# A two-layer local-attention block: another order for the instructions of its steps

## The chip, the core and the metric

The kernel runs on one core of a Trainium2 chip. The metric is the device time of one execution in microseconds; lower is better. A core has four computing engines that each execute their own list of instructions in order: PE (TensorE: matmuls, with weight loads, PEld, beside them), DVE (VectorE), ACT (ScalarE) and POOL (GpSimd). SP (SyncE) issues most DMAs. PE writes to PSUM only; DVE and ACT read PSUM, POOL works on SBUF. Engines wait for one another by semaphores.

## The reference, cut to what matters

The input x is (2, 1024, 256). A first part (attention with 16 heads under conditions, then a soft mixture of 64 experts) and a second part (a rotation of the features, then two layers of local attention with feed-forward) are each added to x. The change touches the second part alone:

```python
def _layer(x, wqkv, qs, ksc, wo, lg, lb, w1, b1, w2, b2):
    h = shift_token(x)
    q, k, v = split(h @ wqkv)                 # 8 heads of 64
    q, k = l2norm(q) * qs, l2norm(k) * ksc
    q, k = rotary_xpos(q, k)
    o = local_attention(q, k, v)              # windows of 128: own and previous one
    x = x + o @ wo
    h = shift_token(x)
    h = (h - mean) / sqrt(var + 1e-5) * lg + lb
    a, g = split(h @ w1 + b1)                 # 682 each
    x = x + (a * gelu(g)) @ w2 + b2
    return x
for l in range(2):
    x = _layer(x, ...)
```

All arithmetic is float32.

## The kernel before, in words

The second block works in windows of 128 tokens: 2 layers x 2 sequences x 8 windows = 32 windows, numbered through. A loop (line 1570 and on) runs over steps s = -2 to 31. In step s the queries, keys and values of window s + 2 are projected, window s + 1's queries and keys are turned to features by rows, window s is scored, exponentiated and divided by its sums, and the weights of windows s - 1 and s - 2 are turned and mixed with the values. Four windows make a chunk of 512 tokens; after its last window follows `project_out`, and the feed-forward of chunk f is spread over four steps by `forward(s - LAG)` with LAG = 7: gates 0 and 1, gates 2 and 3, gate 4 with `centre(f + 1)` and gate 5, then `normalise`, `normalised` and `feed`.

The whole loop stands in `tc.manual_schedule` for PE, DVE, ACT and POOL. So on these engines the instructions are executed in the order in which the Python code issues them; SP's are not in that list. The calls and what they issue:

- `project(i)`: 4 matmuls 128x512, each issued as two instructions (tile pq). `rotate_parts(i)`: ACT copies pq to raw and squares it (sq), DVE multiplies pq with the cosines (t, line 1162), POOL multiplies raw with the sines in two products (t, line 1182).
- `values(i)`: 2 matmuls (pv); `keep_values(i)`: ACT copy to v.
- `norms(i)`: DVE sums the squares (ss) and makes a first guess of the inverse root (z); POOL refines it in 12 small products (nt, zn). `rotated(i)`: DVE adds the two parts of t and multiplies the keys' half with the norms.
- `turn(i)`: 16 half transposes on PE (pt), ACT copies them to qkT, which has slots for three windows.
- `scores(i, hg)`: for each half of the heads, 64-row matmuls (sc). `maxima`: four DVE instructions (line 1268) that add the mask, scale by the queries' norm and find the largest. `weights`: four ACT exponentials with sums. `divide(i, 0)`: a DVE reciprocal and four POOL products; `divide(i, 1)`: the same, all on DVE.
- `turn_e(i, hg)`: 16 half transposes (pe), copied to eT by ACT (hg = 0) or DVE (hg = 1). `mix(i, hg)`: the 64-column matmuls po; after the second half ACT copies po into oT. The tile oT holds one chunk and has one buffer (pool `xin`, bufs = 1).
- `project_out(g)`: 8 matmuls (16 instructions, pwo), then DVE adds to xa and writes xb. `halves(g)`: POOL adds xb's two halves for the mean. `centre(f)`: the mean by PE (pm), two DVE differences (hc), an ACT square, a POOL sum. `gate(f, n)`: matmuls pga, ACT Gelu, DVE product. `feed(f)`: 24 matmul instructions py, then the sums into xa (layer 0) or the output (layer 1).

PSUM tiles of two banks (pq, sc, pe, pt, pwo, pga, py) come from `two_banks`. From the end of the mixture part on it hands out three such tiles in turn: every third from `ps_c`, the others from `ps_b` with two buffers. A tile that comes round again waits until all readers of its last use are done. Single banks (pv, po, pm, pvar) come from `ps_1` with two buffers.

A step is called `dense` (line 1586) when no mixture work stands beside it and it is not one of the last two: s = 5 to 29. Before the change all steps, dense or not, go through one body with conditions. A project_out stands in steps 5, 9, 13, 17, 21, 25 and 29. In step 5 there is no feed-forward yet, in step 6 `centre(0)` and `normalise(0)`. Step 13 also loads tables and projection weights of layer 1 (`weights2(1, "tabs", "wqkv")`), with four POOL products on the tables.

Of the kernel before, what the change touches and what calls it, by code (L numbers as in the profile page):

```python
# [10 lines left out]
F32 = mybir.dt.float32  # L11
# [6 lines left out]
P = 128  # L18
B = 2
# [72 lines left out]
def tile_kernel(ctx: ExitStack, tc: tile.TileContext, a: dict, out: bass.AP):  # L92
# [1003 lines left out]
    with tc.manual_schedule(  # L1096
# [41 lines left out]
        def project(i):  # L1138

            l, b, w = window(i)  # L1140
            pq = two_banks("pq")
            for x in range(2):
                for k in range(2):
                    nc.tensor.matmul(  # L1144
                        pq[:, x, :],
                        shifted(xa, k, b, w * WIN, P),
                        load["wqkv"][:, k, x * 512 : (x + 1) * 512],
                        start=(k == 0),
                        stop=(k == 1),
                    )  # L1150
            pqs[i] = pq.rearrange("p x (h d) -> p (x h) d", d=DH)
# [91 lines left out]
        def scores(i, hg):  # L1243

            at, wins = parts(i)
            lo = 0 if len(wins) > 1 else WIN
            sc = two_banks("sc").rearrange("p x (c k) -> p x c k", c=2)
            for c in range(2):
                for x in range(2):
                    r = slice(64 * x, 64 * x + 64)  # L1250
                    nc.tensor.matmul(  # L1251
                        sc[:, x, c, lo:],
                        qkT[r, 0, 2 * hg + c, i % 3, :],
                        qkT[r, 1, 2 * hg + c, at, :],
                        start=True,
                        stop=True,
                    )
            scs[i, hg] = sc, lo, 2 if len(wins) > 1 and wins[0][1] == i else 0
# [153 lines left out]
        def gate(f, n, between=None):  # L1412

            l = chunk(f)[0]
            if n == 0:
                us[f] = fa["u"]
            pt = two_banks("pga")
            gl = fa["gl"][:, gates[0] % 2, :]
            gates[0] += 1
            if n < NW1:  # L1420
                for x, lo in ((0, W1G + n * P), (1, W1A + n * P)):
                    for k in range(2):
                        nc.tensor.matmul(  # L1423
                            pt[:, x, :], load["w1"][:, k, lo : lo + P], hcs[f][:, k, :], start=(k == 0), stop=(k == 1)
                        )
# [13 lines left out]
            if n == NW1:  # L1439

                nc.gpsimd.tensor_copy(us[f][TG : TG + TAIL, n, :], us[f][:TAIL, n, :])
# [69 lines left out]
                nc.vector.scalar_tensor_tensor(yo, py, col(f"b2{l}", c), yo, ALU.add, ALU.add)  # L1511
                nc.sync.dma_start(out[c * P : (c + 1) * P, b * S + t0 + lo : b * S + t0 + lo + m], yo)

        def forward(at):

            f, k = divmod(at, 4)
            if at == -1:
                normalise(0)
            if not 0 <= f < CHUNKS:
                return  # L1520
            if k == 0:
                gate(f, 0)
                gate(f, 1)
            if k == 1:
                gate(f, 2)
                gate(f, 3)
            if k == 2:
                gate(f, 4)
                if f + 1 < CHUNKS:
                    centre(f + 1)  # L1530
                gate(f, 5)
            if k == 3:
                if f + 1 < CHUNKS:
                    normalise(f + 1)
                    normalised(f + 1)
                feed(f)


# [28 lines left out]

        LAG = 7
        fa = {}
        for s in range(-2, WINDOWS):  # L1570
            now, before, nxt, new = (0 <= s + d < WINDOWS for d in (0, -1, 1, 2))

            if new:
                project(s + 2)
                rotate_parts(s + 2)

            if s == LAG - 1:
                centre(0)
            if s == LAG:
                normalised(0)  # L1580
            ended = 0 <= s - 2 < WINDOWS

            late = s >= WINDOWS - 2
            dense = s > max(PARTS) and not late
            if ended and not dense and not late:
                mix(s - 2, 1)
            if now and dense:
                for hg in range(2):  # L1590
                    scores(s, hg)
            if ended and dense:
                for hg in range(2):
                    if (s - 2, hg) in eTs:
                        mix(s - 2, hg)
            if s == 5:
                rotate(3)
            if now and not dense and not late:
                scores(s, 0)
                maxima(s, 0)  # L1600
            beside(s, "a")
            if before:
                turn_e(s - 1, 0)
            if now and not late:
                if dense:
                    maxima(s, 0)
                weights(s, 0)
            if new:
                values(s + 2)
                keep_values(s + 2)  # L1610
            beside(s, "c")
            if ended and late:
                for hg in range(2):
                    if (s - 2, hg) in eTs:
                        mix(s - 2, hg)
            if now:
                for hg in () if dense else (0, 1) if late else (1,):
                    scores(s, hg)
                for hg in (0, 1) if late else (1,):
                    maxima(s, hg)  # L1620
                    if hg == 0:
                        weights(s, 0)
            if before and not dense:
                mix(s - 1, 0)
            if nxt:
                turn(s + 1)
            if now:
                weights(s, 1)
            if new:
                norms(s + 2)  # L1630
            if s + 2 == B * NWIN - 1:
                weights2(1, "tabs", "wqkv")
            beside(s, "b")
            if 0 <= s - 2 < WINDOWS and (s - 2) % 4 == 3:
                project_out((s - 2) // 4)
                if (s - 2) // 4 in halved:
                    halves((s - 2) // 4)
            if before:
                turn_e(s - 1, 1)
            if now:  # L1640
                divide(s, 0)
            if new:
                rotated(s + 2)
            if s == 5:

                f = xp.tile([P, 4 * NS], F32, tag="e", name="f")
                at = 0
                for name, k, n in (("u", NF, 512), ("w2", NF, D), ("yo", 2, 512), ("rs", 1, 512), ("sq", 2, 512), ("gl", 2, 512)):
                    fa[name] = f[:, at : at + k * n].rearrange("p (k n) -> p k n", k=k)
                    at += k * n  # L1650
                fa["rs"] = fa["rs"][:, 0, :]
                fa["hc"] = xin.tile([P, 2, 2, 512], F32, tag="x1", name="hc")
                load["w2"] = fa["w2"]
                load["w1"] = xp.tile([P, NE // 4 * D], F32, tag="y1", name="w1")[:, : 2 * W1N].rearrange(
                    "p (k n) -> p k n", k=2
                )
                weights2(0, "w1", "w2")
            forward(s - LAG)
            if now:
                divide(s, 1)  # L1660
            beside(s, "e")
            if s == B * NWIN + 2:
                weights2(1, "wo")
            if s == LAG + 4 * (CHUNKS // 2) - 2:
                weights2(1, "w1")
            if s == LAG + 4 * (CHUNKS // 2) - 1:
                weights2(1, "w2")


        w, f = WINDOWS - 1, CHUNKS - 2  # L1670
# [136 lines left out]
```

## Time and profile before

| | us |
|---|---|
| median of 3 runs | 1572.27 (1572.12 to 1572.6) |
| the profiled execution | 1572.25 |
| its span | 1570.2 |
| busy in it: PE, DVE, ACT, POOL | 1553.9, 905.7, 891.9, 539.6 |
| step s = 12 (gates 2 and 3), from its first pq to the next | 18.02 |
| step s = 13 (project_out, gate 4, centre, gate 5) | 24.36 |
| step s = 14 (normalise, feed) | 21.75 |

The steps in the trace are found by the first matmul of pq: s = 5 begins at 968.45, s = 6 at 989.57, s = 12 at 1102.95, s = 29 at 1445.79. A row of the timeline has the start and the duration in us, the engine, the line, the operation, output and inputs by the program's names, partitions x elements and the number of instructions merged; in brackets stands the idle time of the engine before it and who ended it. A row of the waits has who waited for whom, the total in us, how often, and the longest. A merged row's duration ends with the last result, so for how long a group holds PE one takes the start of the next row.

### The profile page before, as it was taken

What the parts mean: (1) busy time and instruction counts of PE and PEld (TensorE: products, weight loads), DVE (VectorE), ACT (ScalarE), POOL (GpSimd) and SP (SyncE); (2) the same over time, 40 slices, a digit from 0 to 9 for tenths busy, and PEclk for the clock granted to TensorE, in tenths of its full rate; (3) what the DMA queues carried; (4) which work ended last, traced back from release to release, by engine and by line L of the source; (5) the groups of instructions that cost most, each with busy time, mean ns of one, the idle gap of its engine ahead of it and who ended that gap; (6) DMA issues with size and microseconds to landing.
All of it is one profiled execution on the core that took longest, in us unless ns stands there. A gap on an engine that the chain in (4) does not pass through costs nothing.

```text
span 1570.2 us, 24701 instructions
## 1 busy us (share of the span) xinstructions
PE 1553.9 (99%) x9664; PEld 762.4 (49%) x9664; DVE 905.7 (58%) x1606; ACT 891.9 (57%) x1678; POOL 539.6 (34%) x835
## 2 busy tenths in 40 slices
PE   8999999999999999999999999999999999999999
PEld 4333433333333444444776666555555554545544
DVE  5868768776873122125455756656575665657532
ACT  2478768787886222226233654766757575666641
POOL 3333323333330100000102345555565555565411
PEclk9999999999999999999999999999999999999999
DMA  5100010000000544445742102000100001000001
GB/s 163 55 14 14 1 21 8 7 15 8 2 1 28 169 144 142 148 158 186 239 122 81 55 1 83 1 1 1 67 2 1 15 1 56 1 1 28 14 14 40
DMA packets 49860, 82.79 MB, mean 53 GB/s; under 512 B 4552, under 2 KB 25200, under 8 KB 49488
## 3 DMA queue, kind: packets, MB, share of 16 engines
q1 hardware_dynamic: 47200, 75.38, 15.6%
q0 software_dynamic: 1584, 5.29, 1.1%
q8 instruction: 76, 1.25, 0.3%
q10 hardware_dynamic: 960, 0.56, 0.1%
q14 instruction: 40, 0.33, 0.1%
HBM read 56.04 MB, written 20.97 MB: 49 GB/s over the span
## 4 chain that ended last, share of the span: by engine, by line
PE 96%; DVE 2%; DMA 1%; ACT 0%; POOL 0%; issue 0%; ACTq 0%; DVEq 0%; POOLq 0%
PE pga L1423 9%; PE sc L344 9%; PE po L362 8%; PE pm L310 7%; PE lg L813 7%; PE cmb L932 7%; PE sl L839 7%; PE pq L1144 6%; PE py L1450 4%; PE pv L1214 4%; PE pwo L1354 4%; PE po L1334 3%; PE sc L1251 3%; PE pe L1229 2%; PE pqk L280 2%; PE py L860 2%
## 5 line engine op out<-in xcount | busy, mean ns | idle before, releaser
L317 DVE TENSOR_REDUCE mx<-pm 128x2 f32<-128x1024 f32 x256 | 301.5, 1220 | 108.0 <-PE pm L310 107.8
L352 ACT ACTIVATE e<-sc 128x512 f32<-128x512 f32 (+1 forms) x500 | 263.6, 613 | 67.7 <-PE pm L310 63.5
L344 PE MATMUL sc<-qs,km 32*128 32x512 f32 x1024 | 247.7, 616 | 0.7 <-ACT cg L562 0.7
L310 PE MATMUL pm<-km,qm 32*128 32x512 f32 x1024 | 242.8, 616 | 0.0
L380 POOL TENSOR_TENSOR ob<-ob,part 128x512 f32<-128x512 f32 x101 | 128.6, 1273 | 251.1 <-ACT part L379 251.1
L1423 PE MATMUL pga<-hc,w 128*128 128x512 f32 x320 | 143.8, 600 | 0.0
L1301 POOL TENSOR_SCALAR e<-e,den 128x256 f32<-128x256 f32 (+1 forms) x128 | 131.2, 1038 | 26.3 <-DVE den L1297 26.2
L362 PE MATMUL po<-e,v 128*32 128x512 f32 x1024 | 136.8, 604 | 0.0
L344 PEld LDWEIGHTS sc<-qs,km 32*128 32x128 f32 x1024 | 91.6, 183 | 86.6 <-ACT e L352 65.2
L1182 POOL TENSOR_TENSOR t<-raw,tabs 128x512 f32<-128x512 f32 x64 | 80.6, 1280 | 142.5 <-ACT raw L1174 142.3
L1285 ACT ACTIVATE e<-e,nmx 128x256 f32<-128x256 f32 (+1 forms) x256 | 123.6, 488 | 3.8 <-DVE nmx L1268 3.5
L932 PE MATMUL cmb<-xb,y 128*128 128x256 f32 x512 | 118.7, 384 | 0.6 <-ACT xb L918 0.6
L1144 PE MATMUL pq<-wqo,xa 128*128 128x512 f32 x256 | 116.4, 597 | 1.9 <-ACT xb L918 1.2
L813 PE MATMUL lg<-phi,xa 128*128 128x512 f32 x256 | 116.1, 595 | 0.0
L839 PE MATMUL sl<-dsp,xb 128*128 128x512 f32 x256 | 114.9, 592 | 0.0
L310 PEld LDWEIGHTS pm<-km,qm 32*128 32x128 f32 x1024 | 83.2, 183 | 49.2 <-DVE mx L317 34.9
L823 DVE TENSOR_TENSOR l<-lg,keep 128x512 f32<-128x512 f32 x32 | 22.1, 692 | 144.8 <-ACT keep L821 144.8
L1268 DVE CUSTOM_DVE_ANT_0 e<-sc,mask,zn 128x256 f32<-128x256 f32 (+1 forms) x256 | 102.0, 462 | 5.4 <-PE sc L1251 5.4
L932 PEld LDWEIGHTS cmb<-xb,y 128*128 128x128 f32 x512 | 94.9, 189 | 17.9 <-issue 3.2
L1174 ACT COPY raw<-pq 128x1024 f32<-128x1024 f32 x32 | 32.4, 1013 | 107.8 <-PE pq L1144 106.7
L1423 PEld LDWEIGHTS pga<-hc,w 128*128 128x128 f32 x320 | 58.9, 190 | 68.0 <-issue 63.8
L821 ACT COPY keep<-lg 128x512 f32<-128x512 f32 x32 | 18.7, 585 | 126.0 <-issue 105.3
(225 smaller groups left out, 2384.1 us busy)
## 6 DMA issues: line engine op xcount, KB each, us to landing
lgd<-keep SPq DMA_DIRECT2D x64, 256.0 KB, 2.4
w<-in_ffn_W SPq DMA_DIRECT2D x16, 1024.0 KB, 7.0
ebig<-lgd SPq DMA_DIRECT2D x64, 256.0 KB, 3.3
wqo<-in_wqkv SPq DMA_DIRECT2D x2, 1536.0 KB, 8.1
w<-in_w SPq DMA_DIRECT2D x2, 1386.0 KB, 6.5
km<-hk SPq DMA_DIRECT2D x32, 64.0 KB, 2.3
qm<-hq SPq DMA_DIRECT2D x32, 64.0 KB, 2.3
phi<-in_phi SPq DMA_DIRECT2D x1, 2048.0 KB, 7.7
```

Of the source, the lines that this page charges most:

```text
L310: nc.tensor.matmul(pm[:, x, :], qm[u % 2][r, i * P : (i + 1) * P], km[u % 3][r, n * 512 : (n + 1) * 512], start=True, stop=True,)
L317: nc.vector.tensor_reduce(mxs[hu][:, i % 4, 2 * half : 2 * half + 2, n], pm, AX.X, ALU.max)
L344: nc.tensor.matmul(sc[:, x, :] if both else sc[x], km[u % 3][r, j * P : (j + 1) * P], qs[u % 2][r, n * 512 : (n + 1) * 512], start=True, s ...
L352: nc.scalar.activation(part, t, AF.Exp, scale=1.0 / HD0**0.5)
L362: nc.tensor.matmul(po[32 * hh : 32 * hh + 32, :], v[b][:, j, at : at + 32], es[s, hh // 2][:, hh % 2, :], start=True, stop=True,)
L380: nc.gpsimd.tensor_tensor(obs[u, n], obs[u, n], part, ALU.add)
L813: nc.tensor.matmul(lg[:, b, :], xa[:, k, b, 1 + m * P : 1 + (m + 1) * P], phi[:, k, n * 512 : (n + 1) * 512], start=(k == 0), stop=(k == 1),)
L839: nc.tensor.matmul(accs[n][b][:, c, :], xo_tm[:, b * 8 + m, c * P : (c + 1) * P], d[:, b, :], start=(m == 0), stop=(m == 7),)
L932: nc.tensor.matmul(acs[q][:, c, :], y[b][:, 4 * jj + j, c * P : (c + 1) * P], eT[:, j // 2, j % 2 * 256 : (j % 2 + 1) * 256], start=(jj == ...
L1144: nc.tensor.matmul(pq[:, x, :], shifted(xa, k, b, w * WIN, P), load["wqkv"][:, k, x * 512 : (x + 1) * 512], start=(k == 0), stop=(k == 1),)
L1301: engine.tensor_scalar(e[:, x, c, lo:], e[:, x, c, lo:], den[:, x, c : c + 1], None, ALU.mult)
L1423: nc.tensor.matmul(pt[:, x, :], load["w1"][:, k, lo : lo + P], hcs[f][:, k, :], start=(k == 0), stop=(k == 1))
```

## The change: what it does

Dense steps get a body of their own, `dense_step(s)`, with another order of the same calls; the loop's old body stays for the other steps. The set-up of the feed-forward's tiles moves into a function, with its place in step 5 kept between divide(s, 0) and forward. In a dense step:

- `values` come right after `project` and `rotate_parts`.
- Then come all transposes: `turn_e(s - 1, 0)`, `turn_e(s - 1, 1)`, `turn(s + 1)`, and `keep_values` after them.
- Then both `scores`, the first maxima and weights, and `mix` of the windows whose weights are turned, also window s - 1, turned in the same step (before: window s - 2).
- Then the second maxima and weights, `project_out` and `halves` where they are due, and only then `norms`.
- `rotated` goes into `forward`, between its two gates or before `feed`.
- `centre(0)` and `normalised(0)` stand ahead of `project`; the loads of step 13 ahead of the scores; `rotate(3)` of step 5 ahead of `values`.

```diff
-        def forward(at):
+        def forward(at, between=lambda: None):
...
             if not 0 <= f < CHUNKS:
+                between()
                 return
             if k == 0:
                 gate(f, 0)
+                between()
                 gate(f, 1)
...
             if k == 2:
                 gate(f, 4)
+                between()
                 if f + 1 < CHUNKS:
                     centre(f + 1)
                 gate(f, 5)
...
+        def dense_step(s):
 
             if s == LAG - 1:
                 centre(0)
             if s == LAG:
                 normalised(0)
+            project(s + 2)
+            rotate_parts(s + 2)
+            if s == 5:
+                rotate(3)
+            values(s + 2)
+            turn_e(s - 1, 0)
+            turn_e(s - 1, 1)
+            turn(s + 1)
+            keep_values(s + 2)
+            if s + 2 == B * NWIN - 1:
+                weights2(1, "tabs", "wqkv")
+            for hg in range(2):
+                scores(s, hg)
+            maxima(s, 0)
+            weights(s, 0)
+            for i in (s - 2, s - 1):
+                for hg in range(2):
+                    if (i, hg) in eTs:
+                        mix(i, hg)
+            maxima(s, 1)
+            weights(s, 1)
+            if (s - 2) % 4 == 3:
+                project_out((s - 2) // 4)
+                if (s - 2) // 4 in halved:
+                    halves((s - 2) // 4)
+            norms(s + 2)
+            divide(s, 0)
+            if s == 5:
+                feed_forward_tiles()
+            forward(s - LAG, lambda: rotated(s + 2))
+            divide(s, 1)
...
             dense = s > max(PARTS) and not late
-            if ended and not dense and not late:
+            if dense:
+                dense_step(s)
+                continue
+            if new:
+                project(s + 2)
+                rotate_parts(s + 2)
...
```

The order in a dense step before, from the code above: project, rotate_parts, scores of both halves, mix of window s - 2, turn_e(s - 1, 0), the first maxima and weights, values, keep_values, the second maxima, turn(s + 1), the second weights, norms, project_out and halves, turn_e(s - 1, 1), divide(s, 0), rotated, forward, divide(s, 1).

More of the change, by code (lines that the diff above doesn't have):

```diff
@@ L1528, in forward @@
                 gate(f, 4)
+                between()
                 if f + 1 < CHUNKS:
@@ L1535, in forward @@
                     normalised(f + 1)
+                between()
                 feed(f)
@@ L1569, in tile_kernel, with feed_forward_tiles @@
         fa = {}
[L1570 to L1575, printed above, removed]
+        def feed_forward_tiles():
+            f = xp.tile([P, 4 * NS], F32, tag="e", name="f")
+            at = 0
+            for name, k, n in (("u", NF, 512), ("w2", NF, D), ("yo", 2, 512), ("rs", 1, 512), ("sq", 2, 512), ("gl", 2, 512)):
+                fa[name] = f[:, at : at + k * n].rearrange("p (k n) -> p k n", k=k)
+                at += k * n
+            fa["rs"] = fa["rs"][:, 0, :]
+            fa["hc"] = xin.tile([P, 2, 2, 512], F32, tag="x1", name="hc")
+            load["w2"] = fa["w2"]
+            load["w1"] = xp.tile([P, NE // 4 * D], F32, tag="y1", name="w1")[:, : 2 * W1N].rearrange(
+                "p (k n) -> p k n", k=2
+            )
+            weights2(0, "w1", "w2")
+        def dense_step(s):
             if s == LAG - 1:
@@ L1580, in tile_kernel @@
                 normalised(0)
-            ended = 0 <= s - 2 < WINDOWS
+            project(s + 2)
[29 more added lines that the diff above has]
+            divide(s, 1)
+            if s == B * NWIN + 2:
+                weights2(1, "wo")
+            if s == LAG + 4 * (CHUNKS // 2) - 2:
+                weights2(1, "w1")
+            if s == LAG + 4 * (CHUNKS // 2) - 1:
+                weights2(1, "w2")
+        for s in range(-2, WINDOWS):
+            now, before, nxt, new = (0 <= s + d < WINDOWS for d in (0, -1, 1, 2))
             late = s >= WINDOWS - 2
             dense = s > max(PARTS) and not late
-            if ended and not dense and not late:
-                mix(s - 2, 1)
[L1589 to L1598, printed above, removed]
+            if dense:
[4 more added lines that the diff above has]
+                rotate_parts(s + 2)
+            ended = 0 <= s - 2 < WINDOWS
+            if ended and not late:
+                mix(s - 2, 1)
+            if now and not late:
                 scores(s, 0)
@@ L1604, in tile_kernel @@
             if now and not late:
-                if dense:
-                    maxima(s, 0)
                 weights(s, 0)
@@ L1616, in tile_kernel @@
             if now:
-                for hg in () if dense else (0, 1) if late else (1,):
+                for hg in (0, 1) if late else (1,):
                     scores(s, hg)
@@ L1622, in tile_kernel @@
                         weights(s, 0)
-            if before and not dense:
+            if before:
                 mix(s - 1, 0)
@@ L1630, in tile_kernel @@
                 norms(s + 2)
-            if s + 2 == B * NWIN - 1:
-                weights2(1, "tabs", "wqkv")
             beside(s, "b")
@@ L1643, in tile_kernel @@
                 rotated(s + 2)
[L1644 to L1657, printed above, removed]
             forward(s - LAG)
@@ L1661, in tile_kernel @@
             beside(s, "e")
[L1662 to L1667, printed above, removed]
         w, f = WINDOWS - 1, CHUNKS - 2
```

## The prediction

> **What bounds the kernel now.** I read the page first: who is busy, and who holds the chain that ended last.
>
> ```profile
> PE 1553.9 (99%) x9664; PEld 762.4 (49%) x9664; DVE 905.7 (58%) x1606; ACT 891.9 (57%) x1678; POOL 539.6 (34%) x835
> PE 96%; DVE 2%; DMA 1%; ACT 0%; POOL 0%; issue 0%; ACTq 0%; DVEq 0%; POOLq 0%
> ```
>
> TensorE sets the end. So the change is worth what it takes out of TensorE's row, less what TensorE must then wait for. Next, TensorE's row for a plain step of the second block (s = 12: start, duration, line, count):
>
> ```profile
> 1102.95 3.60 PE L1144 MATMUL pq<-wqo,xa 128*128 128x512 f32 x8
> 1106.47 2.00 PE L1251 MATMUL sc<-qkT 64*128 64x256 f32 x16
> 1108.40 1.97 PE L1334 MATMUL po<-eT,v 128*64 128x128 f32 x32
> 1110.30 0.71 PE L1229 MATMUL pe<-ident,e 64*128 64x64 f32 x16
> 1110.94 1.98 PE L1214 MATMUL pv<-wqo,xa 128*128 128x512 f32 x4
> 1112.86 0.71 PE L1229 MATMUL pt<-ident,t 64*128 64x64 f32 x16
> 1113.40 0.66 PE L1229 MATMUL pe<-ident,e 64*128 64x64 f32 x16
> 1113.99 7.13 PE L1423 MATMUL pga<-hc,w 128*128 128x512 f32 x16
> 1120.97 0.59 PE L1144 MATMUL pq<-wqo,xa 128*128 128x512 f32 x1
> ```
>
> The step takes 18.02 us without a gap. It uses three shapes of the array: full 128*128, 64*128 (scores, transposes), 128*64 (mix). From the starts of single instructions inside a group, a full matmul takes 0.429 us, a pair of scores 0.216, a mix pair 0.109, a transpose pair 0.062: 28 x 0.429 + 8 x 0.216 + 16 x 0.109 + 24 x 0.062 = 16.97. The missing 1.05 us lies where the shape changes. Third, what the other engines wait for, and the step s = 13, which has a project_out:
>
> ```profile
> POOL nt L1198 <- DVE z L1194: 148.1, 32, 13.1
> DVE xb L1358 <- PE pwo L1354: 55.9, 8, 9.4
> ```
>
> ```profile
> 1131.79 0.22 POOL L1198 TENSOR_TENSOR nt<-z 128x16 f32<-128x16 f32 x1 [3.53 <-DVE z L1194]
> ...
> 1138.69 1.22 DVE L1358 TENSOR_TENSOR xb<-xa,pwo 128x1024 f32<-128x1024 f32 x1 [6.97 <-PE pwo L1354]
> ...
> 1140.18 1.10 POOL L1370 TENSOR_TENSOR f<-xb 128x512 f32<-128x512 f32 x1
> 1140.96 0.17 DVE L1297 RECIPROCAL den<-den 128x4 f32<-128x4 f32 x1
> ...
> 1141.31 4.55 POOL L1301 TENSOR_SCALAR e<-e,den 128x256 f32<-128x256 f32 x4
> ```
>
> The norms on POOL (nt) start 6.9 us before DVE has the project_out sum (xb): they are done under project_out's 16 matmuls. Keep this row in mind.
>
> **What the change removes.** Extra time at a border, from single starts: full to 64*128 before scores 0.199, before transposes 0.145; scores to mix 0.147; mix to transposes 0.150; transposes to full 0.197. Now: pq-sc 0.199, sc-po 0.147, po-pe 0.150, pe-pv 0.197, pv-pt 0.145, pe-pga 0.197 = 1.035. After: pv-pe 0.145, pt-sc, sc-po 0.147, po-pga 0.197 (0.198 at a border po-pga at 1507.1). Transposes directly before scores aren't in the trace. Nearest: feed's 42-row matmuls to transposes at 1487.8, no extra; the far bound is 0.199. I take 0, since both keep 64*128. So 0.546 saved in each of 25 steps (s = 5 to 29), 13.65. In the 7 steps with project_out two more borders go (pt-pwo 0.197, pwo-pe 0.145): 2.4. In step 30 the mix between transposes and scores is gone, 0.35. Together **-16.4 us**; with the far bound -11.4.
>
> [...]
>
> **What it adds.** No instruction is added; all of it is order. Hidden moves: the tabs and wqkv DMAs of s = 13 (and POOL's four tabs products, 4.96 us) now stand before the scores. SP issues the tabs once t2 has read the old ones, 7.3 us into the step, as now; 7.0 for landing and 5.0 give 19.3, and POOL has nothing to do before xb at 19.3. Without that cover each us would be a us. wqkv only gets earlier; the w1/w2/wo DMAs and the xkeep DMA of rotate(3) keep their neighbours. Values one place earlier cost nothing: their bank is freed by v. rotate(3)'s copy on ACT (1.0) goes ahead of the eT copies, while ACT waits for pe. But four waits arise. Below, E is the end of project_out on TensorE.
>
> (a) **Scores behind the eT copy.** The two-bank PSUM tiles go round in a ring of three. The new order is pq, pe, pe, pt, sc, so the first sc takes the tile of the first pe, which ACT must have copied. From the last transpose pair of pe: 0.22 result, 0.04, copy 1.01, 0.145 to TensorE (as from raw's end at 1011.89 to pe at 1012.04) = 1.42; the other two transposes cover 1.05. Wait 0.37, in the 20 steps without a longer wait: **+7.4** (0 if another tile is taken). The scores and all TensorE work queue behind it.
>
> (b) **The norms go behind project_out.** DVE executes in order, and norms(s+2) now follow the xb sum; their POOL half and divide(s,0) follow too. After E: xb 0.18 + 1.22 = 1.4; ss 1.25, z 0.4: 3.05; norms on POOL 4.4 (3.5 when DVE is idle; one of its 0.2 us products takes 1.27 while DVE adds t, as at 1115.57): 7.5; divide 4.16: 11.7. TensorE has gate 3.43, pm 0.86, the last gate 1.72, pq 3.43, pv 1.72, border 0.09: it wants turn_e(s,0) at 11.25, and gets it at 11.85: 0.6. Meanwhile ACT's oT copy waits for E too, since the next group's oT takes the one buffer that project_out reads: oT 0.8, exps 2.8, table load 4.1, gelu 4.8, DVE product 5.5, t sum 6.75, then the product with the norms, 7.5 to 8.2, the two centre differences 9.6, ACT square 10.65, gelu 11.4, DVE product 12.15, divide(s,1) 13.5. turn_e(s,1) wants 12.4, gets 13.65: 1.3. Behind it on DVE the cosines, 14.7, free pq's tile for turn: 14.85 against 14.15: 0.7. Sum 2.6 for s = 9, 13, 17, 21, 25: **+13.0** (with norms of 3.5: 1.85 each, 9.3).
>
> (c) **Step 30** has no pq and pv to cover: turn_e(29,0) wants E + 6.1, gets 11.85: **+5.75**.
>
> (d) **Steps 5 to 7** have no gates. At s = 5 project_out waits for an oT copy behind exps: 0.8. At s = 6 centre(0) moves ahead of pq and waits for xb: 1.55. Then pm, pq, pv end at E + 8.5, divide at 11.7: 3.35. DVE does divide(5,1) to 9.55, centre 10.9; ACT square 12.0, raw 13.05; cosines 14.3; turn at 14.45 instead of 12.9: 1.55. At s = 7: scores end at 17.05, two maxima 19.7, ss and z 21.35, norms 25.8, divide 30.0, while TensorE (mix, pvar, pq, pv) stands at 26.1: 4.0. **+11.3**.
>
> **Sum**: -16.4 + 7.4 + 13.0 + 5.75 + 11.3 = +21. The profiled execution took 1572.25 (span 1570.2 and 2.05 around it), the median is 1572.27, so nothing to correct: **1593 us**.
>
> [...]
>
> **Rivals.** *Other side, nothing waits*: 1572.25 - 16.4 = 1556. It decides if DVE has z done by E - 2.6 (step 30 wants its transposes at 6.1; norms, divide and the way to TensorE take 8.7), that is if ss doesn't queue behind xb, and if the oT copy finds a free buffer. For it: DVE and ACT are busy for only 58 and 57%, TensorE waits nowhere now. Against: the 6.97 us for which DVE waits for pwo, at a place that now stands ahead of ss. *Only (a) remains*, 1563: if TensorE's 5.2 us of pq and pv cover (b) to (d); they do at s = 12, not after E. *Stalls and gains cancel*, 1572: (d) and (c) without (a) and (b). *Heavier*, 1605 to 1615: waits feed on each other (a later z, later POOL, later pe), borders pt-sc cost 0.2 (+5), POOL slows under DVE (divides 4.6: +5). That the change does nothing is excluded: the block is ordered by hand on all four engines, and the rows above follow the code's order.
>
> **Chances.** Forecast 0.70, its own range 1579 (norms 3.5 throughout, (a) nothing) to 1603 (borders +5, divides +5). Heavier 0.10, other side 0.08, only (a) 0.08, cancel 0.04. A measurement of this kernel tells 0.2%, 3 us, from no change. Slower 0.80, same 0.04, faster 0.16. Range 1563 to 1605: it leaves out the other side and most of the heavier case, and the forecast's tail.
>
> **What would show it.** TensorE's row of a plain step should have three borders, some 17.5 us without waits, and sc should wait 0.37 for ACT's eT. pe should wait for POOL e L1301 or DVE e after each project_out, for some 5 to 6 us at step 30, and for 3 to 4 us at steps 6 and 7. POOL nt should start after DVE xb. I am wrong if nt starts before xb there, if TensorE's idle time in the block stays under 16 us, or if borders pt-sc cost.

## The result, and the profile after

The changed kernel takes 1624.17 us (median of 5 runs, 1621.4 to 1624.94), the kernel before 1572.27: a ratio of 1.0329, 95% interval 1.0314 to 1.0344. It is slower, as forecast, but by 52 us and not by 21, and outside the range. The profiled execution took 1624.17 us with a span of 1622.0.

The page of the changed kernel, TensorE's line and the shares of the chain that ended last:

```profile
PE 1570.8 (97%) x9664; PEld 779.1 (48%) x9664; DVE 924.9 (57%) x1606; ACT 894.3 (55%) x1678; POOL 542.5 (33%) x835
PE 87%; DVE 6%; POOL 3%; ACT 2%; issue 1%; DMA 1%; ACTq 0%; POOLq 0%; DVEq 0%
```

The end is still TensorE's, but DVE and POOL now hold 9% of the chain. TensorE also has more busy time (1570.8 against 1553.9 us) with the same 9664 instructions. Waiting gives a part of that at most: a transpose pair behind a wait counts as 0.28 us busy, one in an unbroken row as 0.062, which is some 10 us for the 45 waits of the block. The rest must be instructions that ran slower. Both questions are answered where the forecast put the stops. The three largest of TensorE's waits in the second block (who waits for whom, us in total, times, longest):

```profile
PE pe L1229 <- DVE e L1301: 17.5, 22, 1.1
PE pe L1229 <- POOL e L1301: 11.8, 17, 3.0
PE pt L1229 <- DVE t L1162: 2.7, 5, 1.1
```

TensorE's timeline of step 14, the one behind the project_out of step 13:

```profile
1165.91 3.60 PE L1144 MATMUL pq<-wqo,xa 128*128 128x512 f32 x8
1169.34 1.88 PE L1214 MATMUL pv<-wqo,xa 128*128 128x512 f32 x4
...
1173.23 0.28 PE L1229 MATMUL pe<-ident,e 64*128 64x64 f32 x2 [0.95 <-DVE e L1301]
1173.80 0.27 PE L1229 MATMUL pe<-ident,e 64*128 64x64 f32 x2 [0.30 <-DVE e L1301]
1175.14 0.27 PE L1229 MATMUL pe<-ident,e 64*128 64x64 f32 x2 [1.07 <-DVE e L1301]
1176.40 0.80 PE L1229 MATMUL pe<-ident,e 64*128 64x64 f32 x10 [0.99 <-DVE e L1301]
1176.99 1.06 PE L1229 MATMUL pt<-ident,t 64*128 64x64 f32 x16
1177.85 3.73 PE L1251 MATMUL sc<-qkT 64*128 64x256 f32 x16
```

The second half's weights are handed to TensorE one product at a time, with waits of up to 1.07 us between them. Then the turn of q and k takes 1.06 us where a plain step of this kernel shows 0.66, and the scores 3.73 where it shows 2.00. The same step cut into four stretches (busy us and instructions of each engine, TensorE's granted clock, DMA):

```profile
1165.91:1172.70 6.79, 6.17 (x29) 2.74 (x27) 3.86 (x7) 3.05 (x4) 6.54 (x9) 1.00 0.00 1
1172.70:1175.54 2.84, 0.82 (x6) 0.44 (x6) 2.84 (x4) 1.66 (x2) 2.70 (x4) 1.00 0.01 3
1175.54:1182.37 6.83, 5.96 (x50) 4.79 (x52) 5.52 (x14) 4.25 (x9) 0.66 (x1) 0.50 0.00 0
1182.37:1194.50 12.13, 12.13 (x55) 5.66 (x51) 5.73 (x13) 7.05 (x17) 8.62 (x18) 1.00 0.01 1
```

From 1175.54 on the granted clock is 0.50 for 6.83 us. There are eight such stretches in the block (from 1001.46, 1021.93, 1086.79, 1175.54, 1260.87, 1349.61, 1434.95 and 1520.28), in steps 6, 7, 10, 14, 18, 22, 26 and 30. The kernel before has none: its granted clock is 1.00 in every stretch of the block, also in step 14:

```profile
1145.33:1167.08 21.75, 21.75 (x136) 11.25 (x134) 13.05 (x32) 16.01 (x29) 13.30 (x22) 1.00 0.01 2
```

TensorE is busy for 43.58 of the 54.64 us of the eight stretches. By an estimate from these figures, with work at 0.50 taking up to twice as long (in step 14 a pair of scores 0.426 us for 0.216), that work cost up to 21.8 us more than at full clock.

Why the weights come late stands in DVE's timeline of the same time, and in POOL's:

```profile
1160.10 1.22 DVE L1358 TENSOR_TENSOR xb<-xa,pwo 128x1024 f32<-128x1024 f32 x1 [6.48 <-PE pwo L1354]
...
1171.37 0.74 DVE L1436 SCALAR_TENSOR_TENSOR f<-pga,cols,f 42x512 f32<-42x512 f32 x1 [1.89 <-ACT f L1435]
1172.03 0.16 DVE L1297 RECIPROCAL den<-den 128x4 f32<-128x4 f32 x1
1172.23 4.12 DVE L1301 TENSOR_SCALAR e<-e,den 128x256 f32<-128x256 f32 x4
1176.27 1.21 DVE L1162 TENSOR_TENSOR t<-pq,tabs 128x1024 f32<-128x1024 f32 x1
```

```profile
1162.95 0.22 POOL L1198 TENSOR_TENSOR nt<-z 128x16 f32<-128x16 f32 x1 [0.46 <-DVE den L1297]
...
1171.67 1.26 POOL L1389 TENSOR_TENSOR f<-f 128x512 f32<-128x512 f32 x1
1172.99 0.61 POOL L1441 COPY f<-f 42x512 f32<-42x512 f32 x1
1173.68 2.52 POOL L1182 TENSOR_TENSOR t<-raw,tabs 128x512 f32<-128x512 f32 x2
```

The norms (nt) start after xb, as forecast. But the four products of the second division take 4.12 us, and they end at 1176.35, 0.15 us after POOL's two rotation products. Here POOL is busy throughout, and the single products take 0.85, 0.74, 1.42 and 1.34 us. In the kernel before, such four take 1.15 us in steps in which POOL does nothing beside them (step 12, first row), and 2.16 us in step 27, where the fourth product alone takes 1.37 beside POOL's rotation:

```profile
1104.74 1.15 DVE L1301 TENSOR_SCALAR e<-e,den 128x256 f32<-128x256 f32 x4
...
1413.58 2.16 DVE L1301 TENSOR_SCALAR e<-e,den 128x256 f32<-128x256 f32 x4
...
1414.27 2.60 POOL L1182 TENSOR_TENSOR t<-raw,tabs 128x512 f32<-128x512 f32 x2 [1.59 <-ACT raw L1174]
```

The plain step 12 (four of its rows) is what the forecast said:

```profile
1129.42 1.21 PE L1229 MATMUL pe<-ident,e 64*128 64x64 f32 x32
1130.47 0.66 PE L1229 MATMUL pt<-ident,t 64*128 64x64 f32 x16
1131.25 2.00 PE L1251 MATMUL sc<-qkT 64*128 64x256 f32 x16
1133.17 1.97 PE L1334 MATMUL po<-eT,v 128*64 128x128 f32 x32
```

The step took 17.86 us; 18.02 less 0.546 plus 0.37 would be 17.84. The loss before the scores can be read: from 1130.47 to 1131.25 go 0.78 us for eight transpose pairs of 0.062 (0.50), so the scores start 0.28 us late.

By place, from the starts of the first pq of each step, the forecast against what was measured. The new order mixes one window more in step 5 (1.97 us) that step 30 then lacks, and the short mix of a sequence's first window moves from steps 9, 17 and 25 to 10, 18 and 26 (0.93 each); both shifts are taken out. The forecast of (a), 0.37 us, counts in all steps but the five of the first row.

| steps | forecast, us | measured, us |
|---|---|---|
| 10, 14, 18, 22, 26 | 5 x (2.6 - 0.546) = +10.3 | 142.53 - 106.11 - 2.8 = +33.6 |
| 5 to 7 | 11.3 + 3 x 0.37 - 3 x 0.546 - 0.342 = +10.4 | 69.75 - 54.44 - 1.97 = +13.3 |
| 27 | -0.2 | 20.28 - 18.33 = +1.9 |
| 29 to the last matmul | 5.75 + 0.37 - 0.546 - 0.342 - 0.35 = +4.9 | 125.47 - 120.68 + 1.97 = +6.8 |
| the other 15 | 15 x (0.37 - 0.546) - 5 x 0.342 = -4.4 | -3.3 |

The five stops behind project_out hold 23 of the 31 us that were missed.

### The profile page after: what moved, and what is told of

It is laid out like the page before. It is cut to its first block, busy times and chain, and to the rows that moved or that the text cites. A ratio compares the mean times of both kernels' runs of the same rounds, so it can differ in the third digit from the quotient of the medians.

```text
span 1622.0 us, 24701 instructions
## 1 busy us (share of the span) xinstructions
PE 1570.8 (97%) x9664; PEld 779.1 (48%) x9664; DVE 924.9 (57%) x1606; ACT 894.3 (55%) x1678; POOL 542.5 (33%) x835
## 4 chain that ended last, share of the span: by engine, by line
PE 87%; DVE 6%; POOL 3%; ACT 2%; issue 1%; DMA 1%; ACTq 0%; POOLq 0%; DVEq 0%
PE sc L344 9%; PE po L362 8%; PE pga L1423 8%; PE pm L310 7%; PE lg L813 7%; PE cmb L932 7%; PE sl L839 7%; PE pq L1144 5%; PE sc L1251 4%; PE pwo L1354 3%; PE po L1334 3%; PE py L1450 3%; PE pv L1214 2%; PE pqk L280 2%; PE py L860 2%; DVE e L1301 2%
## 5 line engine op out<-in xcount | busy, mean ns | idle before, releaser
L1301 POOL TENSOR_SCALAR e<-e,den 128x256 f32<-128x256 f32 (+1 forms) x128 | 138.9, 1099 | 18.3 <-DVE den L1297 18.1
L823 DVE TENSOR_TENSOR l<-lg,keep 128x512 f32<-128x512 f32 x32 | 22.1, 692 | 144.8 <-ACT keep L821 144.8
L1436 DVE SCALAR_TENSOR_TENSOR f<-pga,cols,f 128x512 f32<-128x512 f32 (+1 forms) x48 | 35.9, 749 | 93.0 <-ACT f L1435 92.9
```

Source lines behind the costliest of these rows:

```text
L1301: engine.tensor_scalar(e[:, x, c, lo:], e[:, x, c, lo:], den[:, x, c : c + 1], None, ALU.mult)
```

## The experiments

The theory before the runs: the missing time is the late second division, slowed beside POOL, and a half clock that the stops bring. Rivals: the single oT buffer, the place of the norms, or waits alone without a cost of the clock. All kernels are variants of the changed one (1624.2 us) unless said otherwise.

**Norms ahead of project_out again.**

```diff
             weights(s, 1)
+            norms(s + 2)
             if (s - 2) % 4 == 3:
                 project_out((s - 2) // 4)
...
-            norms(s + 2)
             divide(s, 0)
```

> Undoes one part of the change: in all seven project_out steps norms(s+2) is issued ahead of project_out again. Changed kernel: 1624.2 us. The theory (the order makes PE wait, and the waits also pull TensorE's clock down): about 10 us of waits go, because the norms no longer stand behind xb on DVE, and where a stop falls short enough its 6.83 us at half clock goes too, 2.5 us each: 1602 to 1614, with fewer than eight stretches at clock 0.5. Rival, the single oT buffer (ACT's first oT copy of the next chunk behind project_out) makes the wait: 1621 to 1625. Rival, waits alone and no clock effect: 1613 to 1615 with the stretches at 0.5 as before.

Measured: 1606.26 us (1602.87 to 1610.86). That is in the expected span, but not where I had put it. The four runs lie in two groups, near 1603 and 1610 us, and the trace is of the slowest, 1610.86. In it steps 10, 18, 22 and 26 became only 1.0, 1.0, 0.5 and 1.9 us shorter, and step 6 became 6.1 us shorter (19.05 to 12.97, its half clock gone). So the norms make the stop of step 6, and are a small part of these four. There are still eight stretches at half clock, not fewer as expected, but of 44.4 us instead of 54.6. Step 14 became 6.5 us shorter and step 13 4.0 us longer, for a new reason that POOL's timeline shows:

```profile
1147.87 4.95 POOL L1044 TENSOR_TENSOR tabs<-tabs,rows 128x512 f32<-128x512 f32 x4 [6.70 <-DMA tabs<-in_tabs]
1152.78 0.21 POOL L1198 TENSOR_TENSOR nt<-z 128x16 f32<-128x16 f32 x1
...
1156.24 1.09 POOL L1370 TENSOR_TENSOR f<-xb 128x512 f32<-128x512 f32 x1
```

The layer-1 tables, which POOL takes up early in that step and whose DMA it must await, now stand ahead of norms that have become urgent; halves (f<-xb) and the mean on TensorE come 2.1 us late. TensorE then reaches the second half's weights of step 14 at 1167.54, after their division has ended at 1165.10. So the stop of step 14 isn't mended here, it is hidden behind the one of step 13.

**Filler work in the stop.**

```diff
             turn_e(s - 1, 0)
+            if s > 6 and s % 4 == 2:
+                for _ in range(2):
+                    value_products(s + 2)
             turn_e(s - 1, 1)
```

`value_products` issues the matmuls of `values` and allocates nothing.

> Adds work: in steps 10, 14, 18, 22 and 26 the values product of the step is written twice more (8 rows of 0.429 us, 3.43 us a step, 17.2 us in all, the same result into the same bank) between the turns of the first and the second half's weights, where PE now waits 4.3 us for DVE's second division. Theory that the half clock is a cost of its own: the rows fit into the wait, the clock stays at 1.0 there, and the five stretches that follow give back 2.5 us each: 1609 to 1615, although PE has 17 us more to do. Rival, the half clock costs nothing beside the waits: 1623 to 1627. Rival, PE's work sets the end: 1641.

Measured: 1615.52 us (1613.63 to 1618.0), half a microsecond above the expected 1609 to 1615: 8.7 us less with 17.2 us more work. TensorE's timeline of step 14, and the step as one stretch:

```profile
1170.40 3.70 PE L1218 MATMUL pv<-wqo,xa 128*128 128x512 f32 x8
1174.04 0.40 PE L1233 MATMUL pe<-ident,e 64*128 64x64 f32 x6
1174.63 0.53 PE L1233 MATMUL pe<-ident,e 64*128 64x64 f32 x10 [0.20 <-DVE e L1305]
1175.00 0.66 PE L1233 MATMUL pt<-ident,t 64*128 64x64 f32 x16
```

```profile
1164.10:1190.56 26.46, 25.95 (x144) 12.84 (x142) 17.75 (x35) 15.93 (x29) 17.68 (x28) 1.00 0.00 1
```

The clock stays at 1.00, the turn of q and k is back at 0.66, and the step falls from 28.59 to 26.46. The division came no sooner. The half clock is a cost of its own: the five steps fall by 1.7 to 2.1 us each, although 3.43 us of work were added to each. (In this profile step 27, which had none before, got one.)

**The mix after project_out.**

```diff
-            for i in (s - 2, s - 1):
-                for hg in range(2):
-                    if (i, hg) in eTs:
-                        mix(i, hg)
+            mixes = lambda: [mix(i, hg) for i in (s - 2, s - 1) for hg in range(2) if (i, hg) in eTs]
+            if s % 4 != 1 or s == 5:
+                mixes()
...
                 project_out((s - 2) // 4)
...
+                if s > 5:
+                    mixes()
```

> One move: in steps 9, 13, 17, 21, 25 and 29 the values are mixed after project_out, so that ACT's oT copy, and with it the second half's exponentials, no longer stand behind the end of project_out. Theory that the oT copy is a part of the late chain beside the norms: 8.6 us of waits go, and the clock's part of some stops: 1603 to 1616. Theory that the norms behind xb and the second division alone set the stop: 1622 to 1626. The new place adds two borders between kinds of products in each of six steps, at most 2 us in all.

Measured: 1617.68 us (1616.97 to 1618.25), just beyond the expected span, on the side of a smaller effect. The stops got 0.9 to 2.0 us shorter. The oT copy is a part of the chain, not its cause.

**The second division earlier on DVE.**

```diff
-            forward(s - LAG, lambda: rotated(s + 2))
-            divide(s, 1)
+            early = s > 5 and s % 4 == 1
+            forward(s - LAG, lambda: (early and divide(s, 1), rotated(s + 2)))
+            if not early:
+                divide(s, 1)
```

> One move: in steps 9, 13, 17, 21, 25 and 29 the second half's division stands on DVE ahead of the rotation's sum and product, the layer norm's subtraction and the last gate product. In the trace of the changed kernel DVE has 4.6 us with little to do there, and the four products of the division, 0.265 us each in the kernel before, take 4.1 us beside POOL's csum, copy and rotation products. Theory that this late, slowed division is the largest part of the stop: PE waits 4.3 us less in each of five steps, and the stretches at half clock behind them go: 1588 to 1604. Rival, the wait only passes to the cosines and the turn of q and k behind it on DVE: 1615 to 1625.

Measured: 1603.1 us (1602.43 to 1605.3), as expected, and by the medians the largest effect of a single move (the norms first gave 1606.26, with runs from 1602.87). DVE's timeline around the same point of step 13:

```profile
1160.40 0.75 DVE L1436 SCALAR_TENSOR_TENSOR f<-pga,cols,f 128x512 f32<-128x512 f32 x1 [1.74 <-ACT f L1435]
1161.07 0.17 DVE L1297 RECIPROCAL den<-den 128x4 f32<-128x4 f32 x1
1161.27 1.18 DVE L1301 TENSOR_SCALAR e<-e,den 128x256 f32<-128x256 f32 x4
...
1168.51 1.23 DVE L1162 TENSOR_TENSOR t<-pq,tabs 128x1024 f32<-128x1024 f32 x1 [0.29 <-ACT raw L1174]
```

The four products take 1.18 us beside the small products of the norms, and stand ready long before TensorE asks. Steps 10, 14 and 18 fall to 23.4 us with the clock at 1.00; steps 22 and 26 keep a stretch at 0.50, now 3.41 us long. About 1.5 us of waiting stays in each, partly as the rival said: the turn of q and k behind the cosines.

**Without POOL's rotation products in the stop.**

```diff
-            t2 = la.tile([P, 16, DH], F32, tag="t2", name="t2", bufs=1)
+            skip = 11 < i < WINDOWS and i % 4 == 0
+            t2 = ts["t2"] if skip else la.tile([P, 16, DH], F32, tag="t2", name="t2", bufs=1)
...
-            for lo, hi in ((0, hf), (hf, DH)):
+            for lo, hi in () if skip else ((0, hf), (hf, DH)):
```

> The changed kernel without GpSimd's two rotation products of 1.26 us in steps 10, 14, 18, 22 and 26 (windows 12, 16, 20, 24 and 28 keep the sine part of the window before, so they are rotated wrongly); nothing else is taken out. Theory that the second division's products on DVE (0.35 us each alone, 1.34 to 1.42 beside these two) end late because POOL works beside them: the four take about 2.3 us instead of 4.1, PE waits some 1.8 us less in each of five steps, and a part of the half clock goes: 1602 to 1616. Rival, the products are late for their operands or for a semaphore and POOL's work is only beside them: still 4.1 us, 1621 to 1626.

Measured: 1612.12 us (1607.93 to 1613.79), in the expected span. DVE's division in step 14, then POOL's rows beside it:

```profile
1168.34 2.04 DVE L1303 TENSOR_SCALAR e<-e,den 128x256 f32<-128x256 f32 x4
```

```profile
1167.77 1.27 POOL L1391 TENSOR_TENSOR f<-f 128x512 f32<-128x512 f32 x1
1169.10 0.60 POOL L1443 COPY f<-f 42x512 f32<-42x512 f32 x1
```

2.04 us instead of 4.12. The two products that still run beside POOL take 0.85 and 0.74 us, the two that no longer do take 0.34 each. Their operands and their place on DVE are the same, so it is POOL's work beside them that made them slow.

**Two and three moves together.** The first of these kernels takes the edits of the first and third experiment, the second adds that of the fourth.

> Two moves together: norms(s+2) ahead of project_out, and the values mixed after project_out from step 9 on. Alone they brought the changed kernel's 1624.2 us to 1606.3 and 1617.7. Theory that norms and the oT copy are two parts of one late chain on DVE, so that the second counts once the first is gone: 1594 to 1602, and at most five stretches of half clock. Rival, the two are independent and add up: 1599 to 1600. Rival, the chain still ends in the slowed second division on DVE beside POOL, so that the second move brings nothing: 1604 to 1608.

> Three moves together: norms(s+2) ahead of project_out, the values mixed after it, the second half's division ahead of the rotation's sum on DVE. Theory that these three make the whole stop in steps 10, 14, 18, 22 and 26: PE waits under 1 us in each, no half clock there, each of these steps 21.3 to 22.5 us long: 1582 to 1592, the rest above the kernel before (1572.1 us) lying in steps 5 to 7 and 27 to 30. Rival, another wait of 2 us or more takes the place (POOL's first division, or the turn of q and k behind the cosines): 1593 to 1600.

Measured: 1607.42 us (1606.53 to 1608.51) and 1595.37 us (1593.37 to 1595.58). The pair is no faster than the norms alone, as its third expectation had it. With the division moved too, 12 us go, and steps 10, 18, 22 and 26 take 22.95 us at full clock; the total is in the rival's span, but the waiting left in each of these four is 1.0 us, not the rival's 2. The larger rest lay elsewhere: step 7 (24.8 us, half clock), step 13 (28.3, the tables), step 27 (22.2) and the end (124.9, to the last matmul).

**The new order in steps 8 to 28 alone.**

```diff
+            if 8 <= s <= 28:
+                dense_step(s)
+                continue
```

> The kernel before, with the new order and the three moves in steps 8 to 28 alone; steps 5 to 7 and 29 keep the old order. Theory that what is left above the kernel before lies in the steps where the block is entered and left: 1568 to 1575, no half clock. If the new order saves 0.5 us a step in borders as the prediction had it and PE waits only for the eT copy (0.37 us a step) beside it, 1570. Rival, the new order costs in the middle too: 1577 or more.

Measured: 1581.52 us, ratio to the kernel before 1.0063 (1.0049 to 1.0076): 14 us less than with the three moves everywhere. By the steps, 12 of them lay in entering and leaving the new order and 2 in step 13, which is at full clock here. But it is in the rival's span: the middle cost something too. Left there were the turn of q and k behind the cosines in the stops, step 13, and step 27 (22.1 us).

**A split eT copy.** As the last kernel, with one half of each eT copied by ACT and the other by DVE.

```diff
+                nc.scalar.copy(to[:, :n], of[:, :n])
+                nc.vector.tensor_copy(to[:, n:], of[:, n:])
```

> As the kernel with the new order in steps 8 to 28 and three moves, and ACT and DVE each copy one half of each eT (the earlier window's half by ACT, the later by DVE). Theory that the first scores wait for ACT's whole copy, as the prediction's 0.37 us a step says: some 15 such waits go, 3 to 6 us less than the kernel without the split. Rival, the scores wait for the turn of q and k or for DVE's maxima instead: within 1 us of it.

Measured: 1586.31 us, ratio 1.0095 (1.0081 to 1.0108): slower than without. Neither expectation: the waits of TensorE in steps 9 to 28 have a new first line, and DVE's timeline of step 12 shows what is behind it.

```profile
PE sc L1251 <- DVE eT L1321: 5.7, 15, 0.4
```

```profile
1110.02 1.23 DVE L1162 TENSOR_TENSOR t<-pq,tabs 128x1024 f32<-128x1024 f32 x1 [1.14 <-ACT raw L1174]
1111.90 1.29 DVE L1321 COPY eT<-pe 128x512 f32<-128x512 f32 x2 [0.66 <-ACT eT L1320]
```

DVE is done with the cosines at 1111.24 and then stands idle until ACT's half, from 1111.28 to 1111.87, has ended. So the two halves run one after the other: 1.31 us from the start of ACT's to the end of DVE's first, where ACT's whole copy takes 1.01. Why they don't run side by side isn't shown. Step 12 grew by the same 0.30 us (17.86 to 18.16). So the scores do wait for that copy, but this doesn't bring it sooner.

**Each remaining wait mended at its place.**

```diff
-                if f + 1 < CHUNKS:
-                    centre(f + 1)
                 gate(f, 5)
+                if f + 1 < CHUNKS:
+                    centre(f + 1)
...
             norms(s + 2)
+            if s + 2 == B * NWIN - 1:
+                weights2(1, "tabs", "wqkv")
...
+            if s % 4 == 2:
+                divide(s, 1)
```

> From the kernel with the new order and three moves in steps 8 to 28 (1581.5 us), each wait left there taken at its place: in the steps 9, 13, 17, 21, 25 the last gate product goes ahead of the next chunk's centring, so that ACT's copy of q and k, and the cosines behind it, come sooner (1.35 us in steps 10, 18, 22 and 26: 5.4); the second layer's rotation tables are loaded and multiplied after the norms in step 13 (2.4); in the feed-forward steps the second half's division stands ahead of the layer norm (3.9 in step 27, with its half clock). Theory that these are all that is left and the new order then saves its borders: 1567 to 1572, no half clock in the block. Rival, each mended wait hands on to another: 1574 to 1581.

Measured: 1576.89 us, ratio 1.0037 (1.0025 to 1.005): the rival's span. Step 13 fell by 2.4 us (26.46 to 24.07) and step 27 by 4.0 (22.12 to 18.17), as expected. The stops did not shrink (22.89 us), and step 14 grew from 21.59 to 23.68. ACT's timeline at the end of step 9 and the start of step 10 shows why.

```profile
1067.25 1.06 ACT L1387 ACTIVATE f<-hc 128x1024 f32<-128x1024 f32 x1 [4.20 <-DVE hc L1385]
1068.33 1.01 ACT L1174 COPY raw<-pq 128x1024 f32<-128x1024 f32 x1
```

pq was complete at 1066.6, but its copy stands behind the layer norm's square, which waits for DVE; the cosines and the turn of q and k follow (a wait of 1.2 us, 2.0 in step 14).

> From the tidied kernel (1576.9 us) one place is changed: in the steps 9, 13, 17, 21 and 25 DVE's two subtractions of the layer norm go ahead of the rotation's sum, the last gate after both, so that ACT's square no longer stands directly ahead of its copy of q and k; the trace of the tidied kernel has that copy 1.7 us after its products are there, and the turn of q and k waits 1.2 us for the cosines behind it (2.0 in step 14). Theory that this chain over ACT is the last wait of the stop: these steps fall from 22.9 (23.7) us to 21.6, the end gets the 0.9 us back that the tidied kernel lost there: 1567 to 1571. Rival, DVE's own row is too long there: 1574 to 1577.

The edit: in these steps DVE does the two differences before the rotation's sum (gate 4, division, centre, rotated, gate 5).

Measured: 1569.59 us (1568.91 to 1570.92), ratio 0.9989 (0.998 to 0.9998). As expected: steps 10, 18, 22 and 26 take 21.59 us. Step 13 grew by 1.3 us, to 25.39, with 1.1 us of waiting for POOL's halves. This order ends 2 us below the kernel before, a tenth of a per cent, which 11 and 21 runs only just tell apart; it is no gain to build on.

**Only the values moved**, in the kernel before. So that the banks come free, the turn of q and k also goes ahead of the first exponentials.

```diff
                 project(s + 2)
                 rotate_parts(s + 2)
+                if max(PARTS) < s < WINDOWS - 2:
+                    values(s + 2)
+                    keep_values(s + 2)
...
+            if nxt and dense:
+                turn(s + 1)
             if now and not late:
                 if dense:
                     maxima(s, 0)
                 weights(s, 0)
...
```

> The kernel before with one piece of the change in all of steps 5 to 29: the values product directly behind the projection of q and k (and ACT's copies of it and of the turn ahead of the exponentials, so that their banks come free). By the prediction's prices this removes the borders pe-pv (0.197) and pv-pt (0.145) in each step, so 0.342 of the 0.546 us, 8.55 in all; the first gate then takes the tile of a transpose 0.3 us too early for ACT's copy in about half of the steps, and the second half's weights are turned 0.6 us before DVE has read the scores in a few. Plain steps fall from 18.02 and 18.12 us to 17.7 to 17.95: 1563 to 1571. Rival, the borders are not what the rows showed and the values product was a cover for copies: 1572 to 1580.

Measured: 1571.23 us, ratio 0.9996 (0.9987 to 1.0004): no difference that can be told, at the edge between the two expectations. Plain steps fell by 0.09 to 0.16 us, not 0.342. The three largest of TensorE's waits in steps 9 to 28:

```profile
PE pe L1229 <- DVE nmx L1268: 2.1, 4, 0.9
PE pt L1229 <- DVE nmx L1268: 0.8, 1, 0.8
PE pga L1423 <- ACT eT L1321: 0.6, 3, 0.2
```

The borders go, but the product had covered the readers of PSUM tiles: of the 8.55 us, TensorE's idle time in steps 5 to 28 takes back 5.5 (0.41 us before, 5.92 now).

## Why the prediction was right and wrong

- **Direction, and the border term (-16.4)**: right within what the runs tell. With (a), it gives the plain steps to 0.02 us (17.84 forecast, 17.86 measured for step 12), and the 15 undisturbed steps together to 1.1 us. The border pt-sc, taken as 0, costs 0.06: in steps 9, 17 and 25 of the changed kernel, where nothing is waited for there, the scores start 0.062 us after the last transpose pair, as a transpose would, and their first pair takes 0.272 instead of 0.216.
- **(a) Scores behind the eT copy**: mechanism and size right. In step 12 the scores start 0.34 us after the last transpose pair instead of 0.06, and their first pair takes 0.32 instead of 0.216: 0.38 us, for 0.37 forecast. Only the count was too high: in steps 9, 17 and 25, where half as many weights are turned, there is no such wait.
- **(b), the list of times after E**: right up to its last link but one. E is 1159.9; gelu was forecast at 11.4 and came at 11.4 (1171.33), the DVE product at 12.15 and came at 12.2. The step that failed is "divide(s,1) 13.5": it came at 16.4. I had priced it by the rows where POOL rests, some 1.15 us for four products. The trace of before did hold the warning: such a group in step 14 took 1.55 us, its first product 0.77 beside a POOL copy and the others 0.34, and in step 27 a product took 1.37 us beside POOL's rotation, the same two instructions that meet here. I had asked what the moved work would wait for, and what DVE does to POOL (1.27 for a 0.2 us product), but not what POOL does to DVE at the new place. TensorE feels a little less than these 2.9 us: the turn of q and k, forecast at 14.85, starts at 17.1 in steps 14 and 26 and at 17.6 in 10, 18 and 22, which is 12.8 us later in all. The last link, the cosines, cost 0.34 us instead of 0.7, and in steps 14 and 26 nothing.
- **(b), its heading**: "the norms go behind project_out" is not what sets these stops. With the norms first four of them shrink by 0.5 to 1.9 us, with the mix (and so the oT copy) later they shrink by 0.9 to 2.0, with the division first by 3.1 to 5.4, the clock's part in each.
- **The clock**: the rows of before granted 1.00 throughout the block (steps 5 to 29 and on to 1565), and the sum left the clock out. It holds the other part of the miss: between 1.7 us (the least that the filler gave back in one step) and 2.7 (43.58 us of busy time at half clock, divided by two and by eight) in each of eight stops, so some 14 to 22 us. In step 14 no wait was longer than 1.07 us: there are five, 3.50 us in sum with transposes between them, and the clock falls during the last, at 1175.54.
- **(c) and (d)**: the places are right, but for the 0.8 us at s = 5, of which the trace shows no wait. The waits are shorter than forecast: 8.6 us in steps 5 to 7 for 11.3, and 4.7 at the end for 5.75. Three stretches of half clock, up to 8.3 us, more than make up for that, so that these places cost 4.8 us more than forecast. With the old order there (steps 5 to 7 and 29) the three steps are as before, 54.4 us.
- **Missed entirely**: step 27, +1.9 us. It is the same collision: two of its four products take 1.38 and 1.35 us beside POOL's rotation. With the second division of step 26 ahead of the layer norm it goes.
- **Rivals**: "heavier", at 0.10, had the right direction and waits that feed on waits, but it had POOL slowed by DVE and not DVE by POOL, and its 1605 to 1615 lacked the clock. "The other side" fell for the reason given: z came behind xb, and nt started after it (1162.95).

For the five stops the two parts can be added up. The turn of q and k starts 12.8 us later than forecast, and behind it the clock stays at 0.50 for 22.1 us in all, which costs up to 11.0: 23.8 together, for the 23.3 us that were missed there. The two are not independent, since with the division earlier the clock also stayed at 1.00 in three of the five stops (steps 10, 14 and 18) and was at 0.50 for 3.41 us instead of 6.83 in the two others. Of the other 8 us, 4.8 are (c) and (d), 2.1 step 27 and 1.1 the other 15 steps.

## What to carry to other kernels

When work is moved to another place, price it by what runs beside it there, on the other engines too, and not by its row at the old place. On an engine that is busy to 99%, a saving of half a microsecond a step is only worth something if every cover that the moved work gave is counted first. And look at waits in sum: in step 14 five short ones, none over 1.07 us and 3.50 in sum, went with 6.83 us at a granted clock of 0.50, and with filler work put there, which left two of 0.20 us, it stayed at 1.00.

## What the runs showed of the hardware

- A DVE product with one scalar per row (128x256) took 0.33 to 0.35 us alone, up to 0.58 beside POOL's products of the same form, 0.75 to 0.78 beside a POOL copy and 1.34 to 1.42 beside POOL's products of two tensors (the kernels before and after). Without POOL's rotation products, the two that had taken 1.42 and 1.34 took 0.34 each. By which way POOL's work slows DVE's, no run here shows.
- The granted clock fell to 0.50 for 3.41 or 6.83 us. In steps 5 to 28 of the changed kernel it did so in the seven steps in which TensorE's waits came to 3.42 to 3.84 us in sum, and not in steps 5 and 27, with 1.31 and 1.80 us. In other kernels less went with it too: 1.85 us in step 27 of the new order in steps 8 to 28 alone, and about 1.5 us in each of five steps with the division moved, in two of the five.
- A border between transposes and scores, both with 64 rows, costs 0.06 us (steps 9, 17 and 25 of the changed kernel), where the borders with a full matmul cost 0.145 to 0.199 in the kernel before.
